# A feed-forward block on seven products: where the weight checks and the last attention block's normalisation stand

## The chip, the core and the metric

The kernel runs on one core of a Trainium2 chip. The metric is the device time of one execution in microseconds (us), a median over runs; one more execution was taken with the profiler, and all traces and pages come from it. Engines: PE (matrix products), DVE (vector), ACT (activations), POOL, and the queues of SP and POOL that issue most of the DMAs.

## The reference

`x` is 8 x 256 x 256 (batch, tokens, features), `ctx` is 8 x 256 x 256, and a mask marks the valid keys. One causal cross-attention with a residual, then a feed-forward network with a residual; the weights of the network are drawn from -1, 0, 1, each output with a scale:

```python
x = x + attention(layernorm(x), ctx, ctx, mask)       # scores / 16, causal, softmax
y = layernorm(x)
h = silu((y @ w1.T) * s1) * ((y @ w2.T) * s2)         # 256 -> 1024
h = gelu((h @ h1.T) * s3)                             # 1024 -> 1024, exact gelu
h = gelu((h @ h2.T) * s4)                             # 1024 -> 1024
x = x + (h @ w3.T) * s5                               # 1024 -> 256
```

## The kernel before

**Blocks and pairs.** The 2048 tokens go in four blocks of 512 (t = 0 to 3). `pair(s, ...)` takes blocks 2s and 2s+1 through the network together, so that a 1024 x 1024 layer (a "wide layer") can be done with seven products of half-size matrices instead of eight. Each activation is split into a high and a low part (tiles `oh` and `ol`, for the gates' inputs `hyt` and `lyt`): ACT makes the high part by a copy that rounds, DVE the rest by a subtraction (`rest`, L288), and PE multiplies each part. A product takes four output tiles of eight matmuls, 128 x 512 each.

**Units.** `pair` is a generator with 80 units. Units 0 to 7 are the first block's gates: in each, eight matmuls into `pa` and `pb` (L566), the Silu on ACT (`gate`, L578) and the product on DVE (L580, tiles `ha` and `hb`). Units 8 to 11 are product 1 and 12 to 15 product 2 of the first wide layer, 16 to 23 the second block's gates (tiles `hc`, `hd`; DVE also forms the differences T1 and T2 there, L738, whose parts are product 6's input), 24 to 27 product 6, 28 to 31 product 5, 32 to 35 product 3, 36 to 39 product 7, 40 to 43 product 4. Products 1, 6, 5 and 3 add into the banks `px_u`, 7 and 4 into `px_y`, which can start when ACT's GELU (`nc`, L732) has read `px_u`. Units 44 to 71 are the second wide layer, 72 to 79 the last matrix `w3` (L973) with `finish` (L591) and the output's DMA; their split inputs are `oh_po` and `ol_po`. The matrices (matrix n is that of product n) are fetched by POOL's queue (L648), 1 MB each, into three buffers: each fetch waits until the product before the previous two has let its buffer go.

**Attention between the units.** PE's order is written out by hand. `attention(t, ...)` is a generator too; `stages_at` gives a first unit for its loads and then the units after which each next stage is issued, as (pair, (units)). Each engine runs its instructions in that order, so an instruction that waits holds all behind it on its engine. The stages of a late block: statistics of x, their square root, the mean through DRAM, the subtraction, scores (L411) with the bias (L422) and maximum, Exp (L439), transposes of the probabilities (`pp`, L452), their copies (L454, L456), the product with the values (`pv`, L470) added to `xs` (L478), statistics of the result (L248, L249, "mvf"). Then there are two ways to the gates' input. Blocks 0, 1 and the last one normalise tokens on partitions (`normed`: Sqrt, reciprocal, four operations on DVE into `yf`), and PE transposes both `xs` (`pxt`) and `yf` (`pyt`), eight 128 x 128 transposes each (L276). Block 2 takes the other way: Sqrt (L531), reciprocal (L533), then `on_all` (L343): a PE transpose of the statistics (`tmf`, L347), a copy (L349), one DMA to DRAM (L351) and two that bring mean and reciprocal deviation back to all partitions as rows (L355); PE transposes only `xs`, DVE subtracts the mean row (L541), and POOL multiplies with the other row (L542). ACT needs a table load when the next function lies in another set (Sqrt, Silu, Exp, GELU).

**Looks.** The seven-product form is used with weights that are really -1, 0 or 1; the kernel checks that on the way. `look_through` reads all weights once more in 22 pieces of 512 KB (`raw`, L221, by SP's queue, three buffers). Six small pieces (w1, w2, w3) need a maximum on DVE (`seen`, L199); sixteen pieces of the wide layers a Sign on ACT (L203) and a comparison on DVE (L205). Each step of `looking` does the comparison of the piece that was signed in the step before, asks for one new piece, and signs the piece asked for two steps earlier. The new piece takes the buffer of the piece just compared. The list `looks` gives the units of pair 1 after which a step is issued; four steps are issued at units 72, 74, 76 and 78 of pair 0. Unit 61 does what is left. At the end the verdict decides whether a slower exact network is run instead; here it isn't.

Of the kernel before, what the change touches and what calls it, by code (L numbers as in the profile page):

```python
# [48 lines left out]
NBLK = B // NB  # L49
# [18 lines left out]
def network(tc: tile.TileContext, g: Arrays, exact: bool, flag=None):  # L68

    with ExitStack() as ctx:  # L70
        ctx.enter_context(tc.manual_schedule())
        return _network(ctx, tc, g, exact, flag)


def _network(ctx, tc, g, exact, flag):
# [20 lines left out]
    def groups(t):  # L96

        return ((0,), (1,)) if t == 0 else ((0, 1),)
# [7 lines left out]
    def load_block(t, behind=None):  # L106

        xs = new(io, [P, NT, D], "xs", f"xs_{t}", bufs=2)
        kt = new(io, [P, NB, ND, S], "kt", f"kt_{t}", bufs=2)
        vs = new(io, [P, NT, D], "vs", f"vs_{t}", bufs=2)  # L110
        mi = new(io, [P, TB], "mi", f"mi_{t}", I32)
        span = bass.ts(t, TB)
        if behind is not None:
            for tile_ in (xs[:, 0, :1], kt[:, 0, 0, :1], vs[:, 0, :1], mi[:, :1]):
                behind.memset(tile_, 0)
        step = NT if t else 1
        for i in range(0, NT, step):
            nc.sync.dma_start(out=xs[:, i : i + step, :], in_=g.x[t, :, i : i + step, :])
        for n, js in enumerate(groups(t)):
            own = slice(js[0], js[-1] + 1)  # L120
            nc.sync.dma_start(out=kt[:, own], in_=g.ctx_t[t, :, own])
            if n == 0:
                nc.sync.dma_start(out=mi, in_=g.mask[:, span].to_broadcast([P, TB]))
        nc.sync.dma_start(out=vs, in_=g.ctx_n[t])
        return xs, kt, vs, mi
# [25 lines left out]
    def keep_warm(times):  # L151
        if exact:
            return
        warm = ps_mm.tile([P, TB], F32, tag="mm", name="warm")
        for _ in range(times):
            nc.tensor.matmul(warm, lhsT=zeros[:, :P], rhs=zeros[:, :TB], start=True, stop=True)
# [94 lines left out]
    def normed(src, js, mv, y, name):  # L251
        own = tiles(js)
        std = new(work, [P, NT], "std", f"sd{name}", bufs=2)
        nc.scalar.activation(std[:, own], mv[:, 1, own], AF.Sqrt, bias=eps)
        rstd = new(work, [P, NT], "rstd", f"rs{name}", bufs=2)
        nc.vector.reciprocal(rstd[:, own], std[:, own])
        for i in range(NT)[own]:
            nc.vector.tensor_scalar(
                y[:, i, :],
                src[:, i, :],  # L260
                mv[:, 0, i : i + 1],
                rstd[:, i : i + 1],
                ALU.subtract,
                ALU.mult,
            )

    def turned(y, js, name, pool_=None, tag="at"):

        wide = len(js) * S
        room = TB // wide  # L270
        pieces = []
        for c0 in range(0, ND, room):
            pt = (pool_ or ps_at).tile([P, room, wide], F32, tag=tag, name=f"{v}{name}_{c0}")
            for c in range(room):
                for n, i in enumerate(range(NT)[tiles(js)]):
                    nc.tensor.transpose(  # L276
                        pt[:, c, bass.ts(n, P)], y[:, i, bass.ts(c0 + c, P)], ident
                    )
            pieces.append((slice(c0, c0 + room), pt))
        return pieces  # L280
# [14 lines left out]
    def attention(t, result):  # L295

        made = {}

        def once(tag, name, shape, p=work, **kw):
            if name not in made:  # L300
                made[name] = new(p, shape, tag, f"{name}_{t}", **kw)
            return made[name]

        inputs = loaded.pop(t)
        going = [stages(t, js, once, result, *inputs) for js in groups(t)]
        done = object()
        while going:
            going = [stage for stage in going if next(stage, done) is not done]
            yield

    def table(t, js, func):

        if t == 0 and js == groups(t)[-1]:
            nc.scalar.activation(junk, eps, func)

    def near(t):

        return exact or t < 2
# [24 lines left out]
    def on_all(values, tags, name):  # L343

        n = values.shape[1]
        turned_ = ps_at.tile([n * NT, P], F32, tag="at", name=f"{v}t{name}")
        nc.tensor.transpose(turned_, values.rearrange("p n i -> p (n i)"), ident)  # L347
        here = new(work, [n * NT, P], "here", f"h{name}")
        nc.vector.tensor_copy(here, turned_)  # L349
        there = new(rows, [n, TB], "there", name)  # L350
        nc.sync.dma_start(out=there.rearrange("n (i p) -> (n i) p", p=P), in_=here)  # L351
        got = []
        for i, tag in enumerate(tags):
            row = new(work, [P, TB], tag, f"{name}{i}")
            nc.sync.dma_start(out=row, in_=there[i : i + 1].to_broadcast([P, TB]))  # L355
            got.append(row)
        return got
# [43 lines left out]
    def stages(t, js, once, result, xs, kt, vs, mi):  # L401
# [92 lines left out]
        def casts(values):  # L494
            yt.append(once("yth", "hyt", [P, ND, TB], dt=FR))
            if not exact:
                yt.append(once("ytl", "lyt", [P, ND, TB], dt=FR))
            for c, value in values:
                nc.scalar.copy(yt[0][:, c, cols], value)  # L499

        def rests(values):
            for c, value in values if not exact else ():
                rest(yt[1][:, c, cols], value, yt[0][:, c, cols])

        def turned_x():
            pxt = turned(xs, js, f"pxt_{t}_{js[0]}")
            for c, pt in pxt if t else ():
                nc.scalar.copy(xst[:, c, cols], pt)
            return pxt

        if near(t) or t == NBLK - 1:
            y = once("y", "yf", [P, NT, D])
            normed(xs, js, mvf, y, f"f_{t}_{js[0]}")
            table(t, js, AF.Silu)
            yield
            pxt = turned_x()
            if not t and js == groups(t)[-1]:
                keep_warm(WARM_LATER)
            yield
            values = turned(y, js, f"pyt_{t}_{js[0]}", *(() if t else (ps_mm, "mm")))  # L520
            casts(values)
            if t:
                yield
            rests(values)
            if not t:
                yield
                for c, pt in pxt:
                    nc.scalar.copy(xst[:, c, cols], pt)
        else:
            std = once("sq", "sdf", [P, NT], bufs=2)  # L530
            nc.scalar.activation(std, mvf[:, 1, :], AF.Sqrt, bias=eps)  # L531
            yield
            nc.vector.reciprocal(mvf[:, 1, :], std)  # L533
            yield
            mean, rstd = on_all(mvf, ("row", "row2"), f"mf_{t}")
            yield
            turned_x()
            yield
            y = once("y", "yf", [P, ND, TB])
            for c in range(ND):  # L540
                nc.vector.tensor_tensor(y[:, c, :], xst[:, c, :], mean, ALU.subtract)  # L541
                nc.gpsimd.tensor_tensor(y[:, c, :], y[:, c, :], rstd, ALU.mult)  # L542
            yield
            values = [(slice(c, c + 1), y[:, c : c + 1, :]) for c in range(ND)]
            casts(values)
            yield
            rests(values)
# [465 lines left out]
    def at(s, units, action):  # L1013
        for unit in units if isinstance(units, (tuple, list, range)) else (units,):
            plan.setdefault((s, unit), []).append(action)

    def stages_at(t, first_, *places):
        going = []

        def begin():  # L1020
            if t not in loaded:
                loaded[t] = load_block(t)
            going.append(attention(t, ready[t]))

        at(*first_, begin)
        for s, units in places:
            at(s, units, lambda: next(going[0], None))
# [9 lines left out]
    stages_at(  # L1037
        2, (0, 8), (0, (25, 28, 30, 41, 45, 46, 49, 51, 53, 54, 55, 57, 58, 61, 62, 63))
    )
    stages_at(3, (0, 30), (0, (55, 56, 59, 70, 73, 74, 77)), (1, (1, 4, 8, 10, 11, 13)))  # L1040
    at(0, (7, 7, 14, 15), lambda: next(summing[2], None))
    at(0, 9, lambda: sums_from(0))
    at(0, (16, 17, 18, 19), lambda: next(summing[3], None))
# [1 line left out]
    at(0, (32, 33, 34, 37), lambda: next(summing[4], None))  # L1045
    at(0, 44, lambda: w3.extend(load_weight(g.w3t, "w3_")))
    at(0, (72, 74, 76, 78), lambda: next(looking, None))
    looks = (3, 8, 10, 11, 13, 15, 19, 26, 27, 30, 31, 42, 44, 46, 47, 50, 51, 54, 55, 58, 59)
    at(1, looks, lambda: next(looking, None))
    at(1, 61, lambda: [None for _ in looking])  # L1050
    at(1, (66, 70), lambda: next(ending))
# [65 lines left out]
```

## Time and profile before

| | us |
|---|---|
| median of 3 runs (353.94 to 355.0) | 354.73 |
| the profiled execution | 354.44 |
| its span in the trace | 352.7 |
| PE busy | 340.4 |
| DVE busy | 271.6 |
| ACT busy | 218.2 |
| POOL busy | 33.9 |

The clock granted to PE was 0.997 of full speed. Times in the trace are counted from the span's start; the second pair begins at about 190. In the timeline, a line gives the start, the busy time, the engine, the line, the operation, what is written and read, how many, and in brackets the idle time before it and what ended that. The waits of an engine are given as a total, the number of times and the longest.

### The profile page before, as it was taken

Reading aid. Unit: us, or ns where it says so; the run is one execution under the profiler, and the core shown is the slowest. Engines: PE = TensorE matmul, PEld = TensorE weight load, DVE = VectorE, ACT = ScalarE, POOL = GpSimd, SP = SyncE. Lnnn points to the kernel's source line nnn. Section 1 sums busy time; section 2 is a strip of 40 time slices with the busy share of each in tenths; the row PEclk is TensorE's granted clock in tenths of the full one; section 3 lists DMA queues with packets and bytes.
Section 4 is the critical chain, followed back from the end, with each engine's and each line's share of the span. In section 5 each row is a group of like instructions: output and inputs, shape, how many; then the busy total and the mean of one; then the engine's idle time right before and its main releaser. Section 6 shows DMA issues by size and latency. Waiting matters only on the chain.

```text
span 352.7 us, 4329 instructions
## 1 busy us (share of the span) xinstructions
PE 340.4 (97%) x1512; PEld 271.0 (77%) x1512; DVE 271.6 (77%) x416; ACT 218.2 (62%) x298; POOL 33.9 (10%) x73
## 2 busy tenths in 40 slices
PE   8799999999999999999999999999989999999993
PEld 3567888787788888887888878777768888888782
DVE  5768966999799938687987687589967989756771
ACT  3558633548946755757772456456896589766730
POOL 1810000210001410032000000000010000000000
PEclk9999999999999999999999999999999999999998
DMA  6799991899495833469519213930663578740032
GB/s 201 236 334 268 269 334 62 264 336 295 138 391 187 239 121 119 135 236 325 202 61 289 99 59 85 359 132 22 237 239 120 180 270 319 263 161 0 0 109 79
DMA packets 20540, 68.54 MB, mean 194 GB/s; under 512 B 2440, under 2 KB 5280, under 8 KB 16928
## 3 DMA queue, kind: packets, MB, share of 16 engines
q0 software_dynamic: 7488, 36.70, 32.8%
q1 hardware_dynamic: 12880, 31.36, 25.7%
q8 instruction: 14, 0.23, 0.3%
q14 instruction: 14, 0.11, 0.1%
q10 hardware_dynamic: 144, 0.13, 0.1%
HBM read 55.59 MB, written 8.40 MB: 181 GB/s over the span
## 4 chain that ended last, share of the span: by engine, by line
PE 70%; DVE 11%; ACT 5%; DMA 4%; issue 3%; POOL 1%; POOLq 0%; DVEq 0%; ACTq 0%
PE px_u L704 25%; PE px_y L704 15%; PE po L973 8%; PE pa L566 5%; PE pb L566 5%; PE p L704 5%; DMA raw<-h1q 4%; PE ps L411 2%; PE pv L470 2%; DVE ol L288 2%; ACT oh L687 2%; DVE T L738 1%; DVE sign L205 1%; DVE seen L199 1%; DVE hb L580 1%
## 5 line engine op out<-in xcount | busy, mean ns | idle before, releaser
L704 PE MATMUL px_u<-oh,a 128*128 128x512 f32 x256 | 72.5, 398 | 0.0
L704 PE MATMUL px_u<-ol,a 128*128 128x512 f32 x256 | 72.1, 397 | 0.0
L704 PEld LDWEIGHTS px_u<-ol,a 128*128 128x128 f32 x256 | 48.1, 188 | 12.3 <-DVE ol L288 1.1
L704 PEld LDWEIGHTS px_u<-oh,a 128*128 128x128 f32 x256 | 47.7, 188 | 10.8
L578 ACT ACTIVATE gate<-pa,sc 128x512 f32<-128x512 f32 x32 | 22.0, 689 | 26.2 <-PE pa L566 26.0
L704 PE MATMUL px_y<-oh,a 128*128 128x512 f32 x128 | 35.3, 398 | 1.0 <-ACT nc L732 1.0
L704 PE MATMUL px_y<-ol,a 128*128 128x512 f32 x128 | 34.9, 394 | 0.0
L704 PEld LDWEIGHTS px_y<-oh,a 128*128 128x128 f32 x128 | 23.9, 189 | 6.9 <-ACT nc L732 1.4
L704 PEld LDWEIGHTS px_y<-ol,a 128*128 128x128 f32 x128 | 24.1, 188 | 5.6
L648 POOL DMA_DIRECT2D a<-S x16 | 8.5, 530 | 177.8 <-PE px_u L704 54.4
L203 ACT ACTIVATE sign<-raw 128x1024 bf16<-128x1024 f32 x16 | 16.8, 1052 | 10.4 <-DMA raw<-h1q 6.2
L566 PE MATMUL pa<-hyt,w 128*128 128x512 f32 x64 | 20.6, 403 | 1.2 <-ACT hyt L499 0.7
L205 DVE SCALAR_TENSOR_TENSOR sign<-raw,sign 128x1024 bf16<-128x1024 f32 x16 | 19.2, 1221 | 1.2 <-ACT sign L203 1.2
L566 PE MATMUL pb<-hyt,w 128*128 128x512 f32 x64 | 19.9, 391 | 0.3 <-DVE hb L580 0.3
L566 PE MATMUL pa<-lyt,w 128*128 128x512 f32 x64 | 19.9, 392 | 0.1
L566 PE MATMUL pb<-lyt,w 128*128 128x512 f32 x64 | 19.8, 390 | 0.0
L732 ACT ACTIVATE nd<-nd,sc 128x512 f32<-128x512 f32 x16 | 10.7, 716 | 12.3 <-DVE nd L735 12.3
L704 PE MATMUL p<-oh,a 128*128 128x512 f32 x64 | 17.8, 400 | 0.2 <-DVE na L735 0.2
L704 PE MATMUL p<-ol,a 128*128 128x512 f32 x64 | 17.5, 395 | 0.0
L735 DVE TENSOR_TENSOR na<-p,na 128x512 f32<-128x512 f32 x16 | 10.9, 689 | 8.5 <-PE p L704 8.4
L288 DVE TENSOR_TENSOR ol<-nT,oh 128x1024 fp32r<-128x1024 f32 x12 | 14.5, 1221 | 3.9 <-ACT oh L687 3.8
L732 ACT ACTIVATE nb<-nb,sc 128x512 f32<-128x512 f32 x16 | 10.7, 715 | 10.5 <-DVE nb L735 7.9
(168 smaller groups left out, 646.0 us busy)
## 6 DMA issues: line engine op xcount, KB each, us to landing
a<-S POOLq DMA_DIRECT2D x16, 1024.0 KB, 5.3
a<-h1q POOLq DMA_DIRECT2D x6, 1024.0 KB, 7.9
a<-h2q POOLq DMA_DIRECT2D x6, 1024.0 KB, 6.0
raw<-h1q SPq DMA_DIRECT2D x8, 512.0 KB, 4.8
raw<-h2q SPq DMA_DIRECT2D x8, 512.0 KB, 5.1
vs<-ctx_n SPq DMA_DIRECT2D x4, 512.0 KB, 8.2
q<-h1q POOLq DMA_DIRECT2D x4, 512.0 KB, 19.6
q<-h2q POOLq DMA_DIRECT2D x8, 256.0 KB, 14.3
```

The costliest lines, as they stand in the source:

```text
L203: nc.scalar.activation(sign, raw, AF.Sign)
L205: nc.vector.scalar_tensor_tensor(sign, raw, 1.0, sign, ALU.mult, ALU.not_equal, accum_out=count[:, n : n + 1])
L288: nc.vector.tensor_tensor(lo, value, hi.bitcast(F32), ALU.subtract)
L411: nc.tensor.matmul(ps[:, a:e], lhsT=qt[:, c, bass.ts(2 * j + h, P)], rhs=kt[:, j, c, : e - a], start=(c == 0), stop=(c == ND - 1),)
L470: nc.tensor.matmul(pv[:, h, :], lhsT=prt[:, j, bass.ds(a + k * P, P)], rhs=vs[:, 2 * j + k, :], start=(k == 0), stop=(k == n - 1),)
L566: nc.tensor.matmul(pm, lhsT=wc[:, bass.ts(o, P)], rhs=x, start=(n == 0), stop=(n == len(steps) - 1),)
L578: nc.scalar.activation(gate, pa, AF.Silu, scale=sc[:, 0, o : o + 1])
L648: nc.gpsimd.dma_start(out=a, in_=src)
L704: nc.tensor.matmul(bank, lhsT=a[:, k, bass.ts(o, P)], rhs=x[k // 2][part][:, k % 2, :], start=start and (part, k) == steps[0], stop=stop a ...
L732: nc.scalar.activation(out, src, AF.Gelu, scale=sc[:, n, o : o + 1])
L735: nc.vector.tensor_tensor(out, one, other, ALU.add)
L973: nc.tensor.matmul(po, lhsT=w3[j * QK + k][:, bass.ts(o, P)], rhs=xs_[j][k // 2][part][:, k % 2, :], start=(j == 0 and (part, k) == STEPS[0]),
```

## The change

Three lists and a condition change:

- Block 3 goes the way of block 2: the condition that sent the last block to `normed` and the second set of transposes loses its second half, so that `y` is made from transposed `xs` with the rows of `on_all`.
- Block 3's stages: the transposes of the probabilities after unit 75 of pair 0 instead of 77, the product with the values after 77 instead of unit 1 of pair 1, the statistics after 78 instead of (1, 4), the Sqrt after 79; in pair 1 the reciprocal after unit 0, `on_all` after 1, the transposes of `xs` after 5, the subtraction and POOL's products after 8, the high parts after 10, the low parts and the stash of `xst` after 13.
- Looks: units 11, 13, 15, 30, 31 and 59 lose a step, units 1, 5, 12, 14, 16 and 17 get one. Steps 30 and 31 lay in products 5 of the first wide layer; 16 and 17 are the first two units of the second block's gates.

```diff
-        if near(t) or t == NBLK - 1:
+        if near(t):
             y = once("y", "yf", [P, NT, D])
             normed(xs, js, mvf, y, f"f_{t}_{js[0]}")
...
-    stages_at(3, (0, 30), (0, (55, 56, 59, 70, 73, 74, 77)), (1, (1, 4, 8, 10, 11, 13)))
+    stages_at(
+        3, (0, 30), (0, (55, 56, 59, 70, 73, 74, 75, 77, 78, 79)), (1, (0, 1, 5, 8, 10, 13))
+    )
...
-    looks = (3, 8, 10, 11, 13, 15, 19, 26, 27, 30, 31, 42, 44, 46, 47, 50, 51, 54, 55, 58, 59)
+    looks = (1, 3, 5, 8, 10, 12, 14, 16, 17, 19, 26, 27, 42, 44, 46, 47, 50, 51, 54, 55, 58)
     at(1, looks, lambda: next(looking, None))
```

## The prediction

> **What bounds the kernel now.** I read the page first, then the waits of PE, then the timeline around the second pair's start.
>
> ```profile
> span 352.7 us, 4329 instructions
> PE 340.4 (97%) x1512; PEld 271.0 (77%) x1512; DVE 271.6 (77%) x416; ACT 218.2 (62%) x298; POOL 33.9 (10%) x73
> PE 70%; DVE 11%; ACT 5%; DMA 4%; issue 3%; POOL 1%; POOLq 0%; DVEq 0%; ACTq 0%
> ```
>
> PE is busy 97% of the span: an edit pays only by taking work from PE or a wait from its queue. The waits of PE (total, times, longest) are short; of the longest, these three lie in the second pair:
>
> ```profile
> PE px_y L704 <- ACT nc L732: 1.0, 1, 1.0
> PE pa L566 <- ACT gate L578: 0.4, 1, 0.4
> PE pb L566 <- DVE hb L580: 0.3, 1, 0.3
> ```
>
> The timeline shows where they lie, and the transposes that the change drops:
>
> ```profile
> 207.63 0.72 PE L566 MATMUL pb<-hyt,w 128*128 128x512 f32 x2 [0.32 <-DVE hb L580]
> ...
> 216.97 1.03 PE L276 MATMUL pyt<-ident,yf 128*128 128x128 f32 x8
> ...
> 217.76 1.17 PE L704 MATMUL p<-oh,a 128*128 128x512 f32 x4
> ...
> 227.50 1.28 ACT L578 ACT_TABLE_LOAD   x1
> ...
> 229.53 0.73 PE L566 MATMUL pa<-hyt,w 128*128 128x512 f32 x2 [0.42 <-ACT gate L578]
> ...
> 231.75 0.75 DVE L580 SCALAR_TENSOR_TENSOR hc<-pb,sc,gate 128x512 f32<-128x512 f32 x1 [0.83 <-PE pb L566]
> ...
> 260.12 1.04 ACT L203 ACTIVATE sign<-raw 128x1024 bf16<-128x1024 f32 x1
> 261.07 1.99 ACT L687 CAST oh<-hc 128x1024 fp32r<-128x1024 f32 x2
> 262.95 2.41 ACT L732 ACTIVATE nc<-px_u,sc 128x512 f32<-128x512 f32 x4
> ```
>
> Two Signs (257.04 and 260.12) stand on ACT ahead of the GELU that empties px_u, and product 7 starts at 264.26 where PE was free at 263.13. From 264.2 to 347 PE is busy 82.39 of 82.80 us: nothing to gain there.
>
> **What goes, in PE time.** A matmul after a gap loses 0.1 more (the next step is 0.34, not 0.23).
> - Eight transposes of yf: 217.76 − 216.97 + 0.08 = 0.87.
> - pb's wait at 207.63: step 0.71 instead of 0.23, +0.11 = 0.59. It came from DVE, where block 3's statistics (2.2 us, eight instructions from 204.71) stood between the gates. They move ahead of the gates.
> - pa's wait at 229.53: step 0.81, +0.11 = 0.69. It is the Silu load (1.28) behind a Sign that waited 4.5 for its piece. Block 3's Sqrt now runs before the first gates, so no table changes here.
> - px_y's wait: 1.13 + 0.10 = 1.23, if ACT is early enough without the two Signs.
>
> **What comes, the first pair's end.** The scores stay; transposes of the probabilities move from unit 77 to 75 (PE 182.6; Exp had ended at 181.2, no wait), their products from (1,1) to 77, where PE does the same 2.6 us. ACT's copy then stands before the oh_po casts (183.5 to 185.5), DVE's before ol_po (done 187.3); PE wants those at 189.7. DVE goes on: seen 188.4, xs 188.5 to 190.7 with its waits for PE, res 191.75 to 192.45, statistics to 194.64, seen to 195.75, res to 196.5. ACT's Sqrt waits for the statistics till 194.98, with gate 0 queued behind it; Silu load to 196.3, gate 0 to 197.0, ha to 197.78, then the reciprocal (0.18), 197.88. PE reaches the new transpose tmf after unit (1,1) at 193.5 + 3.67 = 197.17, so it waits 0.75, with all of unit 2 behind it. tmf without a wait costs 0.10 (145.13, then a first group of 1.17 for 1.08). Together **+0.85**. Its bounds: 0.10 if DVE is 0.75 earlier than my walk, 1.7 if each of the eight hand-overs between PE, DVE and ACT costs 0.1 more than I put. (pb of unit 1 wants the bank that res frees at 196.5 0.2 earlier; that lies within this wait.) In-order queues: three DMAs join SP at unit (1,1), at 198.9, 200.2 and 200.6 (in block 2 the second was issued 1.26 after the first, landings 3.5 and 4.1): rows there by 204.7. The next weight piece goes out at 201.0 and lands at 205.6 (row 4.6); DVE asks for it at 206.6. yf: two subtractions on DVE, 0.68 each, about 213; on POOL two products, 1.28 and 1.62, to 217.0, ahead of the fetch of matrix 5, whose buffer comes free at 217.1 anyway and which is used at 248. Casts by 217.7, wanted at 224.7. All that costs nothing; without its 7 us of cover the casts would cost PE directly.
>
> So unit 16 starts at 225.28 − 0.87 − 0.59 + 0.85 = **224.67**.
>
> **The second gates.** Three Signs stand between the gates instead of one, and three comparisons on DVE (1.15 each) instead of one. DVE is the tight one: from the third gate's hc at 231.75 to the last rest (244.9) it has hardly any idle time, and product 6 follows its results. So the time of that hc decides. Before it stands, on ACT, the Sign of the piece asked for after unit 14 (call it piece 10), with gates 2 to 7 queued behind. SP may ask for it when DVE has compared piece 7. DVE: p2 starts at 217.15, its adds at 219.4, 221.2, 223.0, comparisons 1.2, rests 1.3: done 224.85. So issue 224.9, with matrix 3 (1 MB) following at 225.1 (in the old trace 0.46 after unit 16's start). Landings of raw pieces:
>
> ```profile
> L221 SPq DMA_DIRECT2D raw<-h2q x1: 328/328/328, 286.5 to 286.5; - x1
> DMA to landing us min/median/max: 5.0/5.0/5.0
> ...
> L221 SPq DMA_DIRECT2D raw<-h2q x1: 328/328/328, 294.9 to 294.9; - x1
> DMA to landing us min/median/max: 5.6/5.6/5.6
> ```
>
> The first was issued 0.6 before a matrix, the second 0.4 after one; two others just ahead of a matrix took 4.5 and 5.1. I take 5.0, since the piece goes first: landing 229.9, Sign to 230.9, gate 2 to 231.6, hc at 231.65, against 231.75 now. The chain behind it is instruction for instruction the same up to hd, and a later piece (asked 228.7, there 233.2, gate 4 by 234.95, hd due at 235.3) doesn't bind. PE ends its gates at 224.67 + 14.68 = 239.35 and waits 0.85 for oh (old end 240.29, now 240.19): the time saved so far is handed back here. Product 6 ends 0.10 earlier than now, and product 7 starts at 263.13 − 0.10 = 263.03 instead of 264.26 + 0.10; the GELU that it needs is done 0.7 earlier by the same rows. **Sum: −1.33.** From there the sum follows the landing us for us, since hc is landing + 1.75: at 5.6 hc stands at 232.25, sum −0.7; at 9.9 (the slowest raw row) at 236.55, sum +3.6. At 3.7 (the fastest) DVE's own queue admits hc at 230.5: −2.4.
>
> The Trainium skill, "DMA: Bandwidth & Descriptors", section Queues, rings and completion order, says that each DMA engine takes the queues with work in turn, packet by packet. By that, piece 10 would share with matrix 3 wherever it stands: an estimate is the lone 3.7 to 4.8 plus 512 KB once more at the 306 GB/s of 217.7 to 225.2, so 5.4 to 6.5, and a sum of −0.9 to +0.3. The rows just ahead of a matrix (4.5, 5.0, 5.1) don't show that.
>
> **The looks elsewhere.** 25 steps as before, all pieces a little earlier, one step fewer in the second layer, where PE doesn't wait: zero. The pieces that used to be read at units 30 and 31 cost nothing where they now stand except as counted.
>
> **Rivals.**
> 1. *Piece 10 comes late.* Place: the Sign before gate 2. The sum is zero at 6.2 us of landing, slower by over 0.3% from 7.3. For it: raw at 159.6 took 9.9 and one asked at 217.18 was signed only at 226.42, both among three other transfers; here the stash of xst and piece 9 are still moving. Against: 12 of the 15 raw landings in the trace are under 6. Say 9.0: +2.7.
> 2. *Piece 10 shares the DMA engines with matrix 3* and takes 5.3 to 7.2: the wait ahead of gate 2 eats what the dropped waits gave, −1.0 to +1.0. For it: 5.3 at 227.3 and 5.6 at 294.9, both asked for after a matrix; 7.0 at 288.3. Against: it goes out first, if my walk of DVE is right to 0.2 us. The rule of turns of the Trainium skill, above, would give this case.
> 3. *The looks leave the middle and px_y waits all the same*, since nc's GELU has only 0.7 to spare: −1.33 + 1.23 = −0.1.
> 4. *The table changes cost more than their rows.* If the Silu load that now stands between Sqrt and gate 0 held ACT for twice its row, PE would wait at tmf 1.28 longer: −0.05. Against: at 227.50 the load took 1.28 and the gate began 0.01 later. The Trainium skill, "ScalarE: Activation LUTs", section What ACT_TABLE_LOAD costs, gives 1283 ns and a drain of 1380 ns for each switch; the trace has the first and not the second.
>
> **Numbers.** The profiled run took 354.44, 1.74 over its span and 0.29 under the median of 354.73; I add the sum to the median: 354.73 − 1.33 = 353.4. What a measurement can tell from no change is about 0.3%, 1.06 us. Faster needs piece 10 within about 5.2: 0.46. Rivals 2, 3 and 4, within 0.3%: 0.25, 0.06 and 0.03. Rival 1: 0.20. The range goes from the fast bound (−2.4: 352.3) to a landing at about 8.1 (+1.9: 356.6); under 2 in 10 lies outside, most of it above.
>
> **What would show it.** Right: no pyt; one table load fewer on ACT; a PE wait of 0.7 at tmf <- DVE mvf; unit 16 about 0.6 earlier; a PE wait of 0.8 at px_u's first oh; no wait at px_y. Wrong: ACT sign waiting for DMA raw by more than 2 us between the gates with pa waiting for gate behind it; px_y still waiting for nc; a wait of the first gates for DVE.

## The result and the profile after

| | before | after |
|---|---|---|
| median of the runs taken with the result, us | 354.87 (6 runs) | 352.68 (6 runs, 352.43 to 353.29) |
| ratio | | 0.9949 [0.9935, 0.9962] |
| the profiled execution, us | 354.44 | 352.55 |
| its span | 352.7 | 350.8 |
| median of a later measurement, on one chip with three more kernels | 354.38 (14 runs) | 353.38 (8 runs, 352.85 to 354.48) |
| ratio | | 0.9976 [0.9961, 0.9991] |

The changed kernel is faster in both, by 0.5% and by 0.2% (−2.19 and −1.00 us); the two intervals touch, hardly more. The forecast was 353.4, from a sum of −1.33. The first median lies near the fast end of its range (352.3). That the second is 353.38 is luck: the kernel before was itself at 354.38 in that measurement, not at the 354.73 from which the forecast started. The page of the changed kernel:

```profile
span 350.8 us, 4320 instructions
PE 338.7 (97%) x1504; PEld 270.0 (77%) x1505; DVE 271.5 (77%) x415; ACT 217.0 (62%) x297; POOL 36.8 (11%) x75
PE 84%; DVE 5%; ACT 2%; issue 1%; POOL 1%; POOLq 0%; ACTq 0%; DVEq 0%
```

PE has eight transposes fewer and one, tmf, more (1512 to 1505 by the weight loads; one matmul record near the start is missing), and ACT has one table load fewer. In the chain that ended last DVE and ACT had 16% together and have 7%. Of PE's waits (total, times, longest), these two are left in the stretch that the change touches; the waits for `nc` (px_y), `gate` (pa) and `hb` (pb) are gone:

```profile
PE tmf L347 <- DVE mvf L533: 0.3, 1, 0.3
PE px_u L704 <- ACT oh L687: 0.2, 1, 0.2
```

The timeline of the changed kernel at the places that the prediction names:

```profile
194.86 1.28 ACT L578 ACT_TABLE_LOAD   x1
196.15 1.27 ACT L578 ACTIVATE gate<-pa,sc 128x512 f32<-128x512 f32 x2
196.32 0.30 PEld L566 LDWEIGHTS pb<-hyt,w 128*128 128x128 f32 x2 [0.53 <-DVE res L591]
...
197.76 0.27 PE L347 MATMUL tmf<-ident,mvf 128*8 128x128 f32 x1 [0.25 <-DVE mvf L533]
...
217.15 1.10 PE L704 MATMUL p<-oh,a 128*128 128x512 f32 x4
...
224.88 10.04 SPq L221 DMA_DIRECT2D raw<-h1q  x4
225.09 0.53 POOL L648 DMA_DIRECT2D a<-S  x1 [6.88 <-PE p L704]
...
229.17 1.06 ACT L203 ACTIVATE sign<-raw 128x1024 bf16<-128x1024 f32 x1 [0.87 <-DMA raw<-h1q]
...
230.85 0.75 DVE L580 SCALAR_TENSOR_TENSOR hc<-pb,sc,gate 128x512 f32<-128x512 f32 x1 [0.41 <-ACT gate L578]
...
239.52 2.12 PE L704 MATMUL px_u<-oh,a 128*128 128x512 f32 x8 [0.22 <-ACT oh L687]
```

There is no pyt before 217.15. Piece 10 was asked for at 224.88, 0.2 ahead of matrix 3, and the trace gives its landing as:

```profile
L221 SPq DMA_DIRECT2D raw<-h1q x1: 328/328/328, 224.9 to 224.9; - x1
...
DMA to landing us min/median/max: 4.2/4.2/4.2
```

Four starts on PE show where the time went. An execution may start earlier or later (below), so each is counted from a product of the first pair ahead of the change, the `p` at 157.38 before and at 157.17 after; the table gives the difference to the kernel before, negative when earlier. w3 is the first `po` of the second pair (331.61 before, 329.51 after). In the forecast's row, product 6 starts at 239.35 + 0.85 = 240.20 and product 7 at 263.03; its −0.10 is said of product 6's end, and the last 0.10 of its −1.33 comes behind product 7's start.

| | unit 16 | product 6 | product 7 (px_y) | w3 |
|---|---|---|---|---|
| forecast | −0.61 | −0.36 | −1.23 | −1.33 |
| changed kernel | −0.45 | −0.83 | −1.78 | −1.89 |
| changed kernel, second trace | −0.46 | −0.61 | −1.55 | −1.66 |
| looks only | −0.03 | +0.20 | −0.70 | −0.54 |
| block 3 only | −0.48 | −1.24 | −1.23 | −0.97 |
| early stages, transposes kept | +0.18 | +0.08 | −0.86 | −0.96 |
| rows, late stages | +2.27 | +2.18 | +1.24 | +1.13 |
| look 14 to 15 | −0.47 | +1.34 | +0.40 | +0.29 |
| look 17 to 18 | −0.46 | −0.32 | −1.27 | −1.37 |
| on_all after unit 2 | −0.85 | −1.04 | −1.93 | −1.76 |
| both of these | −0.85 | −0.72 | −1.62 | −1.45 |
| look 17 to 59 | −0.46 | −1.22 | −2.36 | −2.47 |
| that and on_all after unit 2 | −0.88 | −1.63 | −2.80 | −2.91 |
| that and pair 0's look 78 to 79 | −1.19 | −1.95 | −3.10 | −3.21 |

One thing in the last column is not the edits' doing. From product 7 to w3 most traces take 67.24 (the kernel before 67.35, with the slower step behind px_y's wait). Looks only, on_all after unit 2 and both moves take 67.5, block 3 only 67.6, though PE waits for nothing behind product 7's start: over the whole stretch their matmuls step about 0.2333 instead of 0.2324. The cause isn't known, so where these four are compared, product 6 and product 7 say more than w3.

**Where the two traces of the changed kernel differ.** In the second trace of the changed kernel the whole first pair is 1.17 later than in the first (its `p` at 158.34), and so it is in the run with look 17 at 59. In both, PE waits 0.7 to 0.8 between its first two groups of scores, where the first trace has no wait: the second load of the context (`kt`) landed 6.2 and 6.3 after its issue at 3.54, against 4.8 in the first trace. The timeline of the run with look 17 at 59:

```profile
7.74 1.58 PE L411 MATMUL ps<-kt,qt 128*128 128x128 f32 x8
...
9.98 1.55 PE L411 MATMUL ps<-kt,qt 128*128 128x128 f32 x8 [0.66 <-DMA kt<-ctx_t]
```

and the same place in the first trace of the changed kernel, all sixteen matmuls in one stretch:

```profile
7.52 2.89 PE L411 MATMUL ps<-kt,qt 128*128 128x128 f32 x16
```

Nothing of the change lies there. The two spans differ by 1.91: 1.17 up to the `p`, 0.23 from there to w3, and 0.51 behind the issue of the last output's DMA (5.20 to the end in the first trace, 5.71 in the second, 5.05 to 5.84 over all traces). From the `p` on, the two traces gain 1.9 and 1.7 by w3. This doesn't explain the two medians: the profiled run of the later measurement took 354.45, one of the two slowest of its eight, and how many of the others start or end the late way isn't known, since only profiled runs show it. So the gain is 0.2 to 0.5% by the timed runs and 1.7 to 1.9 us by the traces, and why the medians differ stays open.

### The profile page after: what moved, and what is told of

The parts are those of the page before. It is cut to its first block, busy times and chain, and to the rows that moved or that the text cites. A ratio compares the mean times of both kernels' runs of the same rounds, so it can differ in the third digit from the quotient of the medians.

```text
span 350.8 us, 4320 instructions
## 1 busy us (share of the span) xinstructions
PE 338.7 (97%) x1504; PEld 270.0 (77%) x1505; DVE 271.5 (77%) x415; ACT 217.0 (62%) x297; POOL 36.8 (11%) x75
## 4 chain that ended last, share of the span: by engine, by line
PE 84%; DVE 5%; ACT 2%; issue 1%; POOL 1%; POOLq 0%; ACTq 0%; DVEq 0%
PE px_u L704 34%; PE px_y L704 15%; PE po L973 8%; PE p L704 7%; PE pa L566 7%; PE pb L566 7%; PE ps L411 2%; PE pv L470 2%; PE pxt L276 1%; DVE ol L288 1%; ACT oh L687 1%; PE pp L452 1%; DVE na L735 1%; POOL yf L542 1%; DVE lyt L288 1%
```

## The experiments

### One half each

Looks only (the kernel before with the new list):

```diff
-    looks = (3, 8, 10, 11, 13, 15, 19, 26, 27, 30, 31, 42, 44, 46, 47, 50, 51, 54, 55, 58, 59)
+    looks = (1, 3, 5, 8, 10, 12, 14, 16, 17, 19, 26, 27, 42, 44, 46, 47, 50, 51, 54, 55, 58)
```

> Block 3 as in the kernel before, only the list of looks is the new one. Theory (each part takes away some waits of PE, and the second gates hand some back): the wait of px_y for nc (1.2 us) goes, but the Silu table load before the second gates stays and now three Signs follow it, so pa waits longer for a gate (0.5 to 1.5 us): -0.8 to +0.3 us against the kernel before, and in the trace px_y without a wait and pa <- gate longer than 0.4. Rival (the looks alone make the gain): -1.9 us, as the whole change.

Measured: 353.61 against 354.34, ratio 0.9979 [0.9964, 0.9993]. The timeline of this run:

```profile
228.27 0.75 DVE L580 SCALAR_TENSOR_TENSOR hc<-pb,sc,gate 128x512 f32<-128x512 f32 x1 [2.30 <-ACT gate L578]
...
240.59 2.12 PE L704 MATMUL px_u<-oh,a 128*128 128x512 f32 x8 [0.80 <-ACT oh L687]
```

px_y's wait goes, so it was the Signs of units 30 and 31. But with the old block 3 the Silu load still stands ahead of the second gates, the first hc there waits 2.30 for its gate, and three comparisons instead of one follow: oh is late, and 0.20 is lost at product 6. The loss was expected as a longer wait of pa; pa doesn't wait at all in this trace, px_u waits 0.80 instead.

Block 3 only (the changed kernel with the old list of looks):

```diff
-    looks = (1, 3, 5, 8, 10, 12, 14, 16, 17, 19, 26, 27, 42, 44, 46, 47, 50, 51, 54, 55, 58)
+    looks = (3, 8, 10, 11, 13, 15, 19, 26, 27, 30, 31, 42, 44, 46, 47, 50, 51, 54, 55, 58, 59)
```

> Block 3 by rows with its statistics early, looks as in the kernel before. Theory: no second transposes, no wait of pb in the first gates, no table load before the second gates, a wait at tmf of about 0.4, so unit 16 starts 0.6 us earlier and product 6 about 1 us earlier; px_y still waits about 1 us for nc: -0.8 to -1.3 us against the kernel before. Rival (the looks alone make the gain): 0.

Measured: 353.70, ratio 0.9987 [0.9974, 0.9999], 0.64 less than the kernel before where 0.8 to 1.3 were expected (0.97 less at w3). Its timeline:

```profile
198.45 0.27 PE L347 MATMUL tmf<-ident,mvf 128*8 128x128 f32 x1 [0.25 <-DVE mvf L533]
...
263.52 1.19 PE L704 MATMUL px_y<-oh,a 128*128 128x512 f32 x4 [0.99 <-ACT nc L732]
```

Product 6 is 1.24 earlier, more than in the changed kernel, because only one look is between the gates; px_y's wait then stays at 0.99 and nothing more comes. At product 7 the halves give −0.70 and −1.23, together −1.93; the whole change gives −1.78 and −1.55 in its two traces. They nearly add up: neither is the sole cause.

### What in block 3 pays: the rows or the early stages?

Early stages, but block 3 normalised and transposed as before:

```diff
-        if near(t):
+        if near(t) or t == NBLK - 1:
...
-        3, (0, 30), (0, (55, 56, 59, 70, 73, 74, 75, 77, 78, 79)), (1, (0, 1, 5, 8, 10, 13))
+        3, (0, 30), (0, (55, 56, 59, 70, 73, 74, 75, 77, 78, 79)), (1, (5, 10, 13))
```

> New looks and block 3's scores, products and statistics in their new places, but its y normalised on tokens and transposed by PE as in the kernel before. Theory: PE gets eight transposes back (0.87) and loses tmf with its wait (0.5): about 0.4 us slower than the changed kernel, -1.3 to -1.7 us against the kernel before. Rival (the rows make the gain): 0 to -0.5 us against the kernel before.

Measured: 353.61, ratio 0.9975 [0.9961, 0.9989], 0.73 less than the kernel before: neither the 1.3 to 1.7 expected nor the rival's 0 to 0.5. By the traces it is 0.7 to 0.9 slower than the changed kernel at product 7, not 0.4. tmf and its wait are gone (unit 2 starts 0.44 earlier), but from there to unit 16 it takes 27.90 instead of 26.83, the eight transposes and a second wait of PE for pb's bank, behind `normed` (1.38 on DVE) and the ha that follows it. Rows, but with stages late in pair 1:

```diff
-        3, (0, 30), (0, (55, 56, 59, 70, 73, 74, 75, 77, 78, 79)), (1, (0, 1, 5, 8, 10, 13))
+        3, (0, 30), (0, (55, 56, 59, 70, 73, 74, 77)), (1, (1, 2, 3, 4, 5, 7, 9, 11, 13))
```

> New looks, block 3's y by rows, but the products with the values, statistics and Sqrt after units 1 to 3 of the second pair. Theory: Sqrt and two table loads (1.28 each) stand between the first gates with the statistics' 2.2 us of DVE ahead of them, and PE waits for a gate there: 1.5 to 4 us slower than the changed kernel. Rival (the place of the statistics is of no account, DVE does the same work): as the changed kernel, -1.9 us against the kernel before.

Measured: 357.31, ratio 1.0095 [1.0073, 1.0116], the slowest of all. Its timeline shows why:

```profile
207.83 0.27 PE L347 MATMUL tmf<-ident,mvf 128*8 128x128 f32 x1 [2.77 <-DVE mvf L533]
```

The way by rows has a serial chain (statistics, Sqrt, reciprocal, PE's transpose) that PE meets in its queue. Among the gates, in this order, it costs PE 2.77 of waiting; issued at the end of the first pair it costs 0.25. The wait was expected for a gate; it is for the reciprocal of the statistics. So of the two places tried the rows pay only in the early one; a later `on_all`, with the statistics still among the gates, was not tried. With the early stages unit 16 comes 0.63 earlier by rows (−0.45) than by transposes (+0.18).

### The landing of piece 10

Look 14 issued one unit later, so that piece 10 is asked for later:

```diff
-    looks = (1, 3, 5, 8, 10, 12, 14, 16, 17, 19, 26, 27, 42, 44, 46, 47, 50, 51, 54, 55, 58)
+    looks = (1, 3, 5, 8, 10, 12, 15, 16, 17, 19, 26, 27, 42, 44, 46, 47, 50, 51, 54, 55, 58)
```

> The changed kernel with one look one unit later (after unit 15 instead of 14): piece 10 is asked for about 1.9 us later, its Sign still stands before gate 2. Theory (hc of the third second-block gate is landing + 1.75, and the rest follows it): product 6 starts 1.5 to 1.9 us later, and the kernel is 1.4 to 1.9 us slower than the changed one, about as the kernel before. Rival (the landing of that piece is hidden): no change against the changed kernel, -1.9 us against the kernel before.

Measured: 355.18, ratio 1.0011 [1.0000, 1.0021]; the whole gain is gone. Product 6 is 2.2 later than in the first trace of the changed kernel, a little more than the 1.5 to 1.9 expected. The timeline of this run:

```profile
231.84 1.06 ACT L203 ACTIVATE sign<-raw 128x1024 bf16<-128x1024 f32 x1 [3.19 <-DMA raw<-h1q]
...
233.51 0.75 DVE L580 SCALAR_TENSOR_TENSOR hc<-pb,sc,gate 128x512 f32<-128x512 f32 x1 [2.75 <-ACT gate L578]
233.53 0.73 PE L566 MATMUL pa<-hyt,w 128*128 128x512 f32 x2 [1.15 <-ACT gate L578]
...
242.04 2.12 PE L704 MATMUL px_u<-oh,a 128*128 128x512 f32 x8 [0.96 <-ACT oh L687]
```

This is rival 1's sign: the Sign waits for its piece, and gates, pa and px_u behind it. Five traces in which this Sign stands ahead of gate 2, and which give the piece's landing, show the price (times from the start of unit 16):

| | piece 10 landed | product 6 started |
|---|---|---|
| changed kernel | 4.47 | 14.90 |
| on_all after unit 2 | 4.63 | 15.09 |
| changed kernel, second trace | 4.73 | 15.13 |
| early stages, transposes kept | 4.76 | 15.18 |
| look 14 to 15 | 6.81 | 17.09 |

From the first row to the last the landing is 2.34 later and product 6 2.19: 0.94 us for each us. The first four rows also show how far one trace differs from the next, 4.2 to 4.5 from issue to landing, without any edit to that piece.

### Taking the Sign from ahead of gate 2

The third look of the gates issued after unit 18 instead of 17, so that the Sign of piece 10 stands behind gate 2:

```diff
-    looks = (1, 3, 5, 8, 10, 12, 14, 16, 17, 19, 26, 27, 42, 44, 46, 47, 50, 51, 54, 55, 58)
+    looks = (1, 3, 5, 8, 10, 12, 14, 16, 18, 19, 26, 27, 42, 44, 46, 47, 50, 51, 54, 55, 58)
```

> The changed kernel with the look after unit 17 moved to unit 18: the Sign of piece 10 stands behind gate 2 instead of before it. Theory: hc of the third gate no longer waits (0.41 in the changed kernel), PE's waits at product 6's start (0.22 and 0.34 of steps) shrink: 0.2 to 0.5 us faster than the changed kernel, if the comparison that now follows hc doesn't take it back. Rival (something else sets product 6): no change.

Measured: 353.54, ratio 0.9966 [0.9956, 0.9976]. The third hc no longer waits for ACT, as expected, but the gain isn't there: product 6 is 0.5 later than in the first trace of the changed kernel (−0.32 for −0.83), 0.3 later than in the second. Its timeline:

```profile
230.61 0.75 DVE L580 SCALAR_TENSOR_TENSOR hc<-pb,sc,gate 128x512 f32<-128x512 f32 x1 [1.06 <-PE pb L566]
231.28 1.21 DVE L738 TENSOR_TENSOR T<-hc,ha 128x1024 f32<-128x1024 f32 x1
232.41 1.22 DVE L205 SCALAR_TENSOR_TENSOR sign<-raw,sign 128x1024 bf16<-128x1024 f32 x1
...
237.93 1.22 DVE L738 TENSOR_TENSOR T<-hd,T 128x1024 f32<-128x1024 f32 x1
```

against the changed kernel:

```profile
237.16 1.23 DVE L738 TENSOR_TENSOR T<-hd,T 128x1024 f32<-128x1024 f32 x1
```

The comparison that filled DVE's idle time ahead of this hc (229.21 to 230.43 in the changed kernel) now follows it. Counted from the first pair's `p` (0.26 later in this trace), hc begins 0.50 earlier, DVE idles 1.06 before it, and the T that oh is made from is 0.51 later. So not the start of one hc but all the work on DVE up to that T sets product 6, as soon as the landing doesn't. The run with both moves, below, bears this out: there the piece lands 4.91 after unit 16's start, here 4.34, and product 6 starts 15.41 after it in both.

`on_all` one unit later, to take tmf's wait away:

```diff
-        3, (0, 30), (0, (55, 56, 59, 70, 73, 74, 75, 77, 78, 79)), (1, (0, 1, 5, 8, 10, 13))
+        3, (0, 30), (0, (55, 56, 59, 70, 73, 74, 75, 77, 78, 79)), (1, (0, 2, 5, 8, 10, 13))
```

> The changed kernel with the transpose of the statistics after unit 2 of the second pair instead of unit 1. Theory: PE's wait at tmf (0.4 with its refill) goes and nothing else starts to wait, since the rows are wanted 7 us later: 0.3 to 0.5 us faster than the changed kernel in unit 16's start; product 6 follows DVE's chain, which starts with the gates and so moves too: 0.2 to 0.5 in all. Rival (the rows then come late and POOL's products with them): slower by 0.5 or more.

Measured: 352.86, ratio 0.9949 [0.9931, 0.9967]. tmf's wait is gone and unit 16 0.40 earlier. What is left at product 6 depends on the trace it is compared with: 0.21 of the first of the changed kernel, 0.43 of the second. The difference is piece 10, which took 4.4 from its issue to its landing here and 4.2 and 4.5 there; px_u waits 0.42, against 0.22 and 0.45. At w3 nothing is left against the first trace, for this is one of the traces with the longer steps behind product 7. Both edits together:

> Both moves: the transpose of the statistics after unit 2, and the look after unit 18 instead of 17. Theory: the gains add, 0.4 to 1.0 us faster than the changed kernel, -2.3 to -2.9 us against the kernel before. Rival: no better than one of them alone.

Measured: 353.22, ratio 0.9956 [0.9939, 0.9973]; product 6 is −0.72, no better than the changed kernel. The two don't make a gain together because the moved look is a loss. The move of `on_all` is not: against the run with the moved look alone unit 16 is 0.39 earlier and product 6 0.40. The issue of piece 10 and DVE's work follow unit 16 (the issue comes 0.26 after it in both runs and in the changed kernel), so what is saved ahead of it is kept.

### A version that beats both

If DVE's work decides, a look must leave the gates. The look after unit 17 goes, one after 59 comes back:

```diff
-    looks = (1, 3, 5, 8, 10, 12, 14, 16, 17, 19, 26, 27, 42, 44, 46, 47, 50, 51, 54, 55, 58)
+    looks = (1, 3, 5, 8, 10, 12, 14, 16, 19, 26, 27, 42, 44, 46, 47, 50, 51, 54, 55, 58, 59)
```

> The changed kernel, with the look after unit 17 of pair 1 taken out and one added after unit 59 (as in the kernel before). Between the second gates there are then two Signs and two comparisons instead of three. Theory A (DVE's whole work up to px_u's first oh sets product 6): the wait at px_u (0.22 in the changed kernel, step 0.61 for 0.23) goes, product 6 starts 0.3 to 0.5 earlier counted from the start of the first pair's p product, everything behind it with it: 0.3 to 0.5 us less than the changed kernel. Theory B (what is gained before product 6 is lost further on, at px_y or in the second layer): the wait goes, but px_y waits for nc and the time is the changed kernel's within 0.2 us.

Measured: 352.74, ratio 0.9947 [0.9929, 0.9965], at w3 0.58 less than in the first trace of the changed kernel and 0.81 less than in the second. px_u doesn't wait any more: unit 16 to product 6 takes 14.52, as in block 3 only with its single look, so PE's own work sets it. With `on_all` after unit 2 as well:

> The run before with the rows of block 3 (on_all) issued after unit 2 of pair 1 instead of unit 1. Moving them alone took 0.40 from the start of unit 16 and gave half of it back at px_u's first oh. Theory A: with the third look out of the gates nothing is given back: 0.7 to 0.9 us less than the changed kernel (about 351.8). Theory B: DVE's work still sets product 6, and a wait at px_u of about 0.2 to 0.4 comes back: 0.3 to 0.5 us less than the changed kernel.

Measured: 351.78, ratio 0.9936 [0.9916, 0.9956]; 0.44 less again at w3. At product 6 the move is worth 0.41, as it was with the look after unit 18 (0.40); the landing of piece 10 no longer sets product 6, so it doesn't blur the comparison. With the fourth look of pair 0 moved as well:

```diff
-    at(0, (72, 74, 76, 78), lambda: next(looking, None))
+    at(0, (72, 74, 76, 79), lambda: next(looking, None))
```

> The run before with the fourth look of pair 0 after unit 79 instead of 78, so that DVE adds the last output's residual before it takes the maximum of a small piece. In the changed kernel PE waited at unit 1's pb for that bank (0.27 lost at 196.32). Theory A: those 0.27 go and stay gone: 0.2 to 0.3 us less than the run before. Theory B: the maximum then stands ahead of the reciprocal and of the first ha, the rows come later and PE waits for hb or tmf instead: no gain, within 0.2 us.

Measured: 351.66, ratio 0.9923 [0.9906, 0.9941]; 0.30 less at w3. DVE now frees pb's bank before it takes the maximum:

```profile
194.51 0.73 DVE L591 SCALAR_TENSOR_TENSOR res<-po,s,res 128x512 f32<-128x512 f32 x1
...
195.16 1.21 DVE L199 TENSOR_REDUCE seen<-raw 128x1 f32<-128x1024 uint16 x1
...
238.49 2.02 PE L704 MATMUL px_u<-oh,a 128*128 128x512 f32 x8
```

These three ran beside the changed kernel itself:

> The changed kernel itself, on the same chip as the three runs beside it: 352.7 us and 0.995 of the kernel before by the first measurement.

Measured: 353.38, ratio 0.9976 [0.9961, 0.9991]: the 352.7 and 0.995 were not met again, as told with the result. The interval of the last version and that of its neighbour on the same chip don't meet: [0.9906, 0.9941] against [0.9961, 0.9991]; with the first measurement of the changed kernel, [0.9935, 0.9962], it overlaps. By the traces three moves are worth 1.3 and 1.55 beyond the two of the change. The steps of 0.44 and 0.30 are read from one trace each; by their medians alone the last two versions can't be told apart.

## Why the prediction held, and where it didn't

In short: the waits and transposes that were to go did go, and the wait ahead of product 6 came, as forecast; it was shorter than forecast because piece 10 landed sooner, and so the gain was larger.

- **Unit 16** (−0.61 forecast, −0.45 measured). What goes there was right: from the start of unit 2 to that of unit 16 the kernel before takes 28.30 and the changed one 26.83, 1.47 less for the forecast 0.87 + 0.59. What comes was put at 0.85, all at tmf. It came in two places, 0.91 together: PE first waited at unit 1's pb for the bank that `res` frees (step 0.72 for 0.46, and 0.11 after the gap), which the prediction had counted as lying within tmf's wait; tmf then waited 0.42, with 0.12 for itself and the slower step behind it. The last run's move removed the first, the run with on_all after unit 2 the second. The remaining 0.1 isn't placed. The wait at pb, 0.38 with the gap's price, is one of the prediction's own signs of being wrong ("a wait of the first gates for DVE"), though a small one.
- **The second gates** (product 6's start −0.36 by the forecast's figures, −0.83 measured): this is the term that was mis-sized. From unit 16 to product 6 the forecast had 14.68 of gates and 0.85 of waiting; the two traces have 14.90 and 15.13, of which 0.38 and 0.61 are waiting. The landing was taken as 5.0 and was 4.2 and 4.5; in the first trace hc began at 230.85 instead of 231.65 and the first oh was done at 239.47 instead of 240.19 (0.59 and 0.51 earlier, counted from the `p`). That the issue came at 224.88, forecast for 224.9, is partly luck: counted from the `p` it is 0.19 later, unit 16 being 0.16 late. "From there the sum follows the landing us for us" was right: 0.94 in the five traces. So was the floor that it gave, DVE's own queue (230.5; in the trace the comparison ahead of hc ends at 230.43). It doesn't say that this comparison costs as much behind hc as ahead of it; the look moved to unit 18 found that.
- **The end of product 6** (−0.10 forecast) was reckoned from the first oh, done at 240.29 before and at 240.19 by the forecast, as if product 6 had waited for oh before the change. It had not: oh was done 0.27 ahead of it. This cost the sum little, by luck: product 6 runs some 0.2 longer when it starts after a wait (22.75 to product 7, against 22.56 in the run with look 17 at 59, where px_u doesn't wait), which the forecast left out. The two lines of the kernel before:

```profile
239.24 1.05 ACT L687 CAST oh<-T 128x1024 fp32r<-128x1024 f32 x1 [0.52 <-DVE T L738]
...
240.56 2.02 PE L704 MATMUL px_u<-oh,a 128*128 128x512 f32 x8
```

- **Product 7** (−1.23 forecast, −1.78 measured). The wait of 1.13 is gone, as forecast, so rival 3 is out: looks only shows that the Signs were its cause, block 3 only that it stays with them. The stretch from product 6 is 0.95 shorter; the forecast's 240.20 to 263.03 make it 0.87. From product 7 to w3 it is 0.1 less, the gap's price that the forecast had.
- **Rival 1** (piece 10 late) did not happen, but the mechanism is real and its price is as said: the landing 2.34 later cost the whole gain. By the prediction's sum a landing 6.6 after the forecast's issue, as in that run, gives about +0.25; the trace has +0.29 at w3.
- **Rival 2** (shared DMA engines). In ten traces piece 10 goes out 0.2 to 0.3 ahead of matrix 3. It took 4.1 to 4.6 in them, within the lone rows' 3.7 to 4.8; matrix 3 took 6.4 to 6.9. The rule of turns in the Trainium skill, "DMA: Bandwidth & Descriptors", section Queues, rings and completion order, gave an estimate of 5.4 to 6.5 for the piece; the measurement decides against this use of it. Where matrix 3 went first, by 1.6 (look 14 at 15), it took 4.9 and the piece 4.7; in the kernel before, with the same lead, 5.6 and 5.3.
- **Rival 4** (table changes). The load between Sqrt and gate 0 took 1.28, from 194.86, and the gate began at 196.15. The drain of 1380 ns in the Trainium skill, "ScalarE: Activation LUTs", section What ACT_TABLE_LOAD costs, is not seen here either.

The sum fell short of the traces by 0.56 and 0.33 at w3. Nearly all of it lies between unit 16 and product 6, which is 0.63 and 0.40 shorter than forecast because piece 10 landed 0.79 and 0.53 sooner; unit 16 itself gave 0.16 and 0.15 back. The sign was right because the three waits and the transposes that were to go did go.

## What to carry to other kernels

Put a serial chain that PE must meet (statistics, root, reciprocal, transpose) where PE still has queued work of another kind: the same rows cost 0.25 of waiting at the end of one pair and 2.77 among the next pair's gates. Background work in an in-order queue is paid where that engine's result is wanted next, so count its whole work up to that result before it is moved: the gates took two looks free of charge (14.52 from unit 16 to product 6, as with one), and the third cost 0.4 to 0.6. And compare a small move more than once: moving `on_all` seemed to be worth 0.21 at product 6 against one trace of the changed kernel and 0.43 against the other, because a DMA's landing varied between them; in the two pairs of runs in which that landing didn't set product 6 it was worth 0.40 and 0.41.

## What was not expected of the hardware

- Of two overlapping transfers on different queues the second in issue paid when they were 0.2 to 0.3 apart: the piece took 4.1 to 4.6, the matrix 6.4 to 6.9. With the matrix 1.6 ahead they took 4.9 and 4.7 in one trace, 5.6 and 5.3 in the kernel before, where the matrix ahead of it was still moving. No run varied the gap on purpose, so it stays open whether order or gap is the cause.
- The same program starts in more than one way: PE's first scores waited 0.7 to 0.8 for the first loads in two traces and not in the others beside them, and the first pair then ran 1.2 later. In a kernel where edits are worth 0.3 to 1 us, two traces are compared from a point ahead of the edit, not from the span's start.
